# Tokenizer of a vision tower: the first two linear layers as one product of 512 columns over raw pixels and their std, with the weights loaded and combined ahead of the images

## The chip, the cores and the metric

The kernel runs on one core of one Trainium2 chip. A core has five engines that run side by side: TensorE (PE; its weight loads are shown as PEld), VectorE (DVE), ScalarE (ACT), GpSimd (POOL) and SyncE (SP), and 16 DMA engines that work off the transfers which SP, ACT and POOL issue. The metric is device time in microseconds; the time of a kernel is the median of its runs. All data is float32, and each matrix product of the program is two instructions on TensorE.

## The reference

Four images of 3 x 224 x 224 are cut into 8 x 8 patches: 784 tokens per image, 3136 in all, of 192 values each. What matters here is the tokenizer:

```python
def layernorm(x, g, b):
    mu = jnp.mean(x, axis=-1, keepdims=True)
    var = jnp.mean(jnp.square(x - mu), axis=-1, keepdims=True)
    return (x - mu) * jax.lax.rsqrt(var + EPS) * g + b
...
tokens = layernorm(patches, ln1_g, ln1_b)
tokens = tokens @ W1 + b1
tokens = layernorm(tokens, ln2_g, ln2_b)
q = tokens
k = tokens
tokens = jnp.concatenate([q, k, tokens], axis=1)
h1 = layernorm(tokens @ Wp1 + bp1, lnp_g, lnp_b)
h1 = jax.nn.silu(h1)
return h1 @ Wp2 + bp2
```

W1 is 192 x 256, Wp1 and Wp2 are 256 x 256, and EPS is 1e-5. The three copies of the tokens are equal, so the kernel computes one and writes it three times at the end. Behind the tokenizer come an attention over the images, a mixture of six experts with two chosen per token, a linear attention and a second mixture of four experts. The diff doesn't touch those.

## The kernel before

The 3136 tokens are 28 tiles of 112 rows (TT), taken in 7 groups of 4 tiles (GT). Inside a `manual_schedule` block the engines it names issue in the order in which the code is written; everywhere else, and for the engines not named, a planner chooses the order from modelled costs.

**Loading.** Lines 208 to 219 allot `img` (112 partitions, which are image and patch row; 32 rows of 224 pixels, of which 24 are pixels and 8 are zeros) and issue the four images by turns on SP and ACT, then the gain and shift of the first normalisation (ACT) and W1 (SP). Line 228 and the next load b1, spread over the partitions (POOL), Wp1 (SP) and bp1 (POOL). The small vectors of all layers are gathered as rows of `stage` by POOL (line 170) and turned into columns `cols` by one transpose (line 446). SP then loads the other weights and, once POOL has cleared `nothing` (line 249), writes zeros over `xrows` and `yrows` in device memory (line 253): 38 transfers of 1024 KB and two of 768.

**Turning the patches.** `turn_patches(k)` (line 342) turns 4 of the 28 patch columns: 32 small products against the identity per half, two halves, and a ScalarE copy into `pT` for each. After it VectorE takes the statistics of the same 4 columns (line 443). Ahead of k = 5 `first_layer` (line 357) multiplies the gain into W1, takes the mean over its rows off, adds the shift's part to b1 and permutes the rows of W1 to the order of `pT`. After k = 6 `patch_scales` (line 397) makes 1/std of every patch and brings it, by one product (`pr`, line 415), to the layout of the tokens. All of it is written in order for VectorE and TensorE (line 425).

**The tokenizer.** `tokenize(g)` (line 499) is a pipeline of three steps over groups. Step 1 for group g: the product with W1 (`pw`), times 1/std plus b1, statistics, rescaled rows `xn`. Step 2 for group g - 1: `turned_rows` transposes `xn` and applies ln2's gain and shift on ScalarE (`xTln_g`), the product with Wp1 (`pwp`), plus bp1, statistics, rescaled rows. Step 3 for group g - 2: transpose, lnp's gain and shift and Silu on ScalarE (`xTlnp_g`), the product with Wp2 (`pwp`), plus bp2 into `h`. Every product goes through `mm_rows` (line 312; its matmuls are at line 317), every transpose through `transposed` (line 292; line 297). Products use seven PSUM buffers of 512 columns in turn. Groups 0 to 6 are called at line 528, in the planner's order; `tokenize(7)` and `tokenize(8)`, which finish the last groups, stand in the hand-written block of line 1040, on either side of `keys_values(0)`. That function (line 1016) makes the attention's keys and values of a group (`pkv`), and `second_norm` the statistics it needs.

## Time and profile before

| | |
|---|---|
| median of 3 runs | 815.91 us (812.31 to 816.7) |
| profiled execution | 849.85 us |
| its span | 848.1 us |
| mean granted TensorE clock in it | 0.954 |
| busy in the span: PE, DVE, ACT, POOL | 88%, 61%, 38%, 15% |
| images landed, TensorE starts on them | 17.2 us |
| first product of the tokenizer | 39.3 us |
| first transposes for the keys | 136.4 us |

The profile is of one execution, and that one took longer than the runs. A row of the timeline gives start, length, engine, source line, operation, output and inputs, the number of instructions merged, and in brackets how long the engine sat idle before it and what ended that. "Line 317" is a helper's line, so products are told apart by their tiles. The page's table of 40 slices shows in its DMA row that the DMA engines are nearly saturated from the start until about 125 us: at first by the images and weights, then by the zeros.

### The profile page before, as it was taken

How to read it: one execution, taken by the hardware profiler on the slowest of the kernel's cores; microseconds unless marked ns; L12 is line 12 of the kernel's file. 1: busy time of each engine (PE TensorE's matmuls, PEld its weight loads, DVE VectorE, ACT ScalarE, POOL GpSimd, SP SyncE). 2: the span in 40 equal slices, each digit the busy share in tenths (PEclk: the TensorE clock that was granted, in tenths of full speed). 3: DMA queues.
4: the chain of work that ended last, by engine and by line, in shares of the span. 5: the costliest groups of instructions: out<-in, count | busy, mean ns of one | idle time of the engine just before them, and what ended most of it. 6: DMA issues, size and time to landing. Idle time of an engine off the chain costs nothing. (4 is left out here: it accounts for less than half of the span.)

```text
span 848.1 us, 11129 instructions
## 1 busy us (share of the span) xinstructions
PE 746.0 (88%) x3669; PEld 525.4 (62%) x3669; DVE 515.1 (61%) x1619; ACT 318.2 (38%) x758; POOL 129.3 (15%) x151
## 2 busy tenths in 40 slices
PE   2879988999788788799999999348999999999996
PEld 2758765555465466678878885335767675555553
DVE  4369886585787874346445655358995745544441
ACT  1333535455547573242222323323564612222221
POOL 5100000000024605430030022744000000000000
PEclk9999999999999988799999999759999999999999
DMA  8999990000001293332342224311000001333333
GB/s 197 360 421 419 419 384 0 1 0 1 1 22 55 82 367 95 103 127 75 100 131 88 94 88 137 93 52 55 1 2 0 1 3 27 100 101 101 99 100 100
DMA packets 58286, 97.52 MB, mean 115 GB/s; under 512 B 14590, under 2 KB 48564, under 8 KB 53364
## 3 DMA queue, kind: packets, MB, share of 16 engines
q1 hardware_dynamic: 51100, 80.78, 27.7%
q0 software_dynamic: 6224, 14.13, 5.8%
q10 hardware_dynamic: 904, 1.89, 0.9%
q8 instruction: 29, 0.48, 0.2%
q14 instruction: 29, 0.24, 0.1%
HBM read 31.04 MB, written 65.74 MB: 114 GB/s over the span
## 5 line engine op out<-in xcount | busy, mean ns | idle before, releaser
L901 POOL DMA_INDIRECT xrows<-xn,pos x56 | 59.9, 1070 | 282.4 <-ACT kq L665 233.2
L1369 POOL DMA_INDIRECT ys<-yrows,pos x56 | 54.3, 969 | 163.5 <-DMA yrows<-yb 134.0
L1173 PE MATMUL pb<-xTb,own 128*128 128x256 f32 x240 | 60.3, 396 | 7.0 <-DVE hb L1181 2.1
L1190 PE MATMUL pyb<-own,hb 128*128 128x256 f32 x240 | 59.4, 392 | 4.4 <-ACT hb L1179 4.4
L1173 PE MATMUL pb<-hb,own 128*128 128x256 f32 x240 | 58.8, 388 | 0.3 <-DVE hb L1181 0.3
L1179 ACT ACTIVATE hb<-pb,own 128x256 f32<-128x256 f32 x74 | 34.7, 473 | 61.7 <-PE pb L1173 42.1
L1173 PEld LDWEIGHTS pb<-xTb,own 128*128 128x128 f32 x240 | 45.5, 198 | 16.7 <-ACT xTb L1163 3.8
L1190 PEld LDWEIGHTS pyb<-own,hb 128*128 128x128 f32 x240 | 46.9, 197 | 12.0 <-ACT hb L1179 5.2
L297 PE MATMUL pt<-ident,xn 112*128 112x112 f32 x280 | 42.2, 281 | 12.4 <-DVE xn L482 6.9
L1574 PE MATMUL pqk<-Wqkv,lxT 128*112 128x512 f32 x112 | 50.0, 595 | 0.5 <-ACT lxT L81 0.5
L297 PEld LDWEIGHTS pt<-ident,xn 112*128 112x128 f32 x280 | 32.4, 148 | 26.4 <-issue 9.1
L1173 PEld LDWEIGHTS pb<-hb,own 128*128 128x128 f32 x240 | 44.5, 195 | 6.2 <-DVE hb L1181 0.7
L1196 DVE TENSOR_TENSOR yb<-pyb,eb 128x512 f32<-128x512 f32 x30 | 20.7, 691 | 45.5 <-PE pyb L1190 35.3
L306 PE MATMUL pe<-xT,eW 128*128 128x448 f32 x112 | 45.2, 546 | 0.0
L1648 PE MATMUL pukx<-xa,uk 112*128 112x258 f32 x112 | 29.0, 415 | 18.5 <-ACT uk L1606 18.5
L1163 ACT COPY xTb<-ptb 128x512 f32<-128x512 f32 x30 | 17.5, 583 | 73.8 <-PE ptb L1159 65.2
L1181 DVE TENSOR_SCALAR hb<-pb,own 128x256 f32<-128x256 f32 x46 | 22.2, 482 | 30.9 <-PE pb L1173 29.6
L1648 PEld LDWEIGHTS pukx<-xa,uk 112*128 112x128 f32 x112 | 22.7, 208 | 22.3 <-issue 18.8
L317 PE MATMUL pwo<-Wo,oT 128*112 128x256 f32 x112 | 29.0, 413 | 7.6 <-DVE oT L730 6.7
L1574 PEld LDWEIGHTS pqk<-Wqkv,lxT 128*112 128x112 f32 x112 | 19.2, 177 | 25.2 <-issue 22.7
L690 DVE SCALAR_TENSOR_TENSOR prod<-kq 128x784 f32<-128x784 f32 x32 | 30.4, 971 | 7.2 <-ACT kq L665 5.0
L1582 ACT ACTIVATE qk<-qk 112x256 f32<-112x256 f32 x56 | 22.8, 407 | 28.1 <-DVE qk L1578 23.8
(339 smaller groups left out, 1525.4 us busy)
## 6 DMA issues: line engine op xcount, KB each, us to landing
xrows<-nothing SPq DMA_DIRECT2D x19, 1024.0 KB
yrows<-nothing SPq DMA_DIRECT2D x19, 1024.0 KB
out_dram<-h SPq DMA_DIRECT2D x26, 336.0 KB
xb<-xrows SPq DMA_DIRECT2D x30, 256.0 KB
yrows<-yb SPq DMA_DIRECT2D x30, 256.0 KB
ew<-in_L_ffn_expert_w_dram SPq DMA_DIRECT2D x6, 768.0 KB
wb<-wd SPq DMA_DIRECT2D x28, 112.0 KB
img<-in_x_dram ACTq DMA_DIRECT2D x2, 588.0 KB
```

Source lines behind the costliest of these rows:

```text
L297: nc.tensor.transpose(pt[:, j * TT : (j + 1) * TT], xn[:, j, c * P : (c + 1) * P], ident[:TT, :TT])
L306: nc.tensor.matmul(pm[: wcols.stop - wcols.start, :n], w[:, c, wcols], xT(c), start=(c == 0), stop=(c == chunks - 1),)
L317: nc.tensor.matmul(pm[:, i, :], xT(c, t), w[:, c, :], start=(c == 0), stop=(c == chunks - 1))
L690: nc.vector.scalar_tensor_tensor(prod, qTs[s][:, o, :], 1.0, kT[:, o, t * SEQ : (t + 1) * SEQ], ALU.mult, ALU.mult, accum_out=atts[s][:, o ...
L901: put = nc.gpsimd.indirect_dma_start(out=xrows[:, :], out_offset=bass.IndirectOffsetOnAxis(ap=pos[:, k, t0 + j : t0 + j + 1], axis=0), in_ ...
L1173: nc.tensor.matmul(pm, wm[:, c, o * P : (o + 1) * P], src[:, c, :], start=(c == 0), stop=(c == 1),)
L1179: nc.scalar.activation(dst[:, o, :], pm, AF.Relu, bias=b)
L1190: nc.tensor.matmul(pm[:, t, :], src[:, c, t * P : (t + 1) * P], wm[:, c, :], start=(c == 0), stop=(c == 1),)
L1369: got = nc.gpsimd.indirect_dma_start(out=y[:, j, k, :], out_offset=None, in_=yrows[:, :], in_offset=bass.IndirectOffsetOnAxis(ap=pos[:, k, ...
L1574: nc.tensor.matmul(pqk, xT[:, c, cut(j, 1)], Wqkv[:, c, : 2 * D], start=(c == 0), stop=(c == 1),)
L1582: nc.scalar.activation(half, half, AF.Square, accum_out=ss[:, j, i : i + 1])
L1648: nc.tensor.matmul(pg, uks[u][:, k, c * P : (c + 1) * P], xas[u % 4][:, k, : D + 2], start=(j == 0), stop=(j == TPI - 1),)
```

## The change

The normalisation of a patch is (x - mean) / s with s = sqrt(var + 1e-5). The mean is already taken off through the weights. Now s is left in, too: the product of raw pixels with the first weights is s times what it was, b1 has to be multiplied by s, and the next normalisation takes s out again, if its epsilon is scaled by s squared. So each patch's s is written as one more row of `img` (row 24, pixel 7 of the patch), where `turn_patches` turns it along with the pixels, and b1 becomes the matching row of the weights. Then ln2's gain and mean are multiplied into Wp1 as well and both layers are combined: `Wall` holds W1's 256 columns, which serve only to take ln2's variance, and the 256 columns of W1 times Wp1.

- Loads: ln1, ln2, W1, b1 and Wp1 are issued on SP and ACT ahead of the images; bp1 on POOL ahead of the small vectors. ln2 leaves `stage`.
- `first_layers` replaces `first_layer`; it stands ahead of the first `turn_patches`, and also combines the two weights.
- `patch_stds(k)` stands ahead of `turn_patches(k)`, which now needs the std of its columns; `scaled_variances` takes the place of `patch_scales`.
- `first_rows` replaces steps 1 and 2: one product of 512 columns per tile, of which ScalarE copies the right half into `y` and VectorE takes statistics of the left; then scale and bp1 on `y`, statistics, rescaled rows. `y` has two buffers instead of one.
- The transposes and the evacuation of step 2 go. Silu's transposes of group g - 1 stand in iteration g, its third product in iteration g + 1, so `tokenize(8)` holds only a product.

The parts of the diff that carry it (removed functions are in the listing above):

```diff
+    tok = ctx.enter_context(ExitStack())
+    tokp = tok.enter_context(tc.tile_pool(name="tok", bufs=1))
+    bp1 = tokp.tile([TT, D], F32, tag="bp1", name="bp1")
+    nc.gpsimd.dma_start(out=bp1, in_=a["L0_tok_bp1"].partition_broadcast(TT))
...
+    ln1 = tokp.tile([2, PD], F32, tag="ln1", name="ln1")
+    ln2 = tokp.tile([4, P], F32, tag="ln2", name="ln2")
+    b1 = tokp.tile([1, D], F32, tag="b1", name="b1")
+    W1 = tokp.tile([KP, 2, D], F32, tag="W1", name="W1")
+    Wp1 = tokp.tile([P, 2, D], F32, tag="Wp1", name="Wp1")
+    nc.sync.dma_start(out=ln1[:1], in_=a["L0_tok_ln1_g"].unsqueeze(0))
+    nc.scalar.dma_start(out=ln2[:2], in_=a["L0_tok_ln2_g"].rearrange("(r p) -> r p", p=P))
+    nc.sync.dma_start(out=ln1[1:], in_=a["L0_tok_ln1_b"].unsqueeze(0))
+    nc.scalar.dma_start(out=ln2[2:], in_=a["L0_tok_ln2_b"].rearrange("(r p) -> r p", p=P))
+    nc.sync.dma_start(out=W1, in_=a["L0_tok_W1"].rearrange("(s p) n -> p s n", p=KP))
+    nc.scalar.dma_start(out=b1, in_=a["L0_tok_b1"].unsqueeze(0))
+    nc.scalar.dma_start(out=Wp1, in_=a["L0_tok_Wp1"].rearrange("(c p) n -> p c n", p=P))
     for b in range(NI):
         eng = nc.scalar if b % 2 else nc.sync
...
+    SROW = 3 * 32 + CY
...
+    def without_mean(w, n, dim):
+        pm = ps_tile("pmean")[:n, :D]
+        for i in range(2):
+            nc.tensor.matmul(pm, allones[:n, :n], w[:, i, :], start=(i == 0), stop=(i == 1))
+        for i in range(2):
+            nc.vector.scalar_tensor_tensor(
+                w[:, i, :], pm, -1.0 / dim, w[:, i, :], ALU.mult, ALU.add
+            )
+    def first_layers():
+        gb = tokp.tile([P, 8], F32, tag="gbT", name="gbT")
         pt = ps_tile("pgb")
+        nc.vector.memset(gb, 0.0)
         for i in range(2):
             nc.tensor.transpose(
                 pt[:KP, 2 * i : 2 * i + 2], ln1[:, i * KP : (i + 1) * KP], ident[:2, :2]
             )
+        nc.tensor.transpose(pt[:, 4:8], ln2, ident[:4, :4])
+        nc.vector.tensor_copy(gb[:KP, :4], pt[:KP, :4])
+        nc.vector.tensor_copy(gb[:, 4:], pt[:, 4:8])
+        g1, g2 = (lambda i: gb[:KP, 2 * i : 2 * i + 1]), (lambda c: gb[:, 4 + c : 5 + c])
+        bb = tokp.tile([P, 2, TT], F32, tag="bb", name="bb")
         W1g = tokp.tile([KP, 2, D], F32, tag="W1g", name="W1g")
+        W2 = tokp.tile([P, 2, D], F32, tag="W2", name="W2")
         for i in range(2):
+            nc.vector.tensor_scalar(W1g[:, i, :], W1[:, i, :], g1(i), None, ALU.mult)
+        without_mean(W1g, KP, PD)
+        pw = ps_tile("pbw")[:1, :D]
         for i in range(2):
             nc.tensor.matmul(
+                pw, gb[:KP, 2 * i + 1 : 2 * i + 2], W1[:, i, :], start=(i == 0), stop=(i == 1)
             )
         nc.vector.tensor_tensor(b1, pw, b1, ALU.add)
         pp = ps_tile("pwc").rearrange("p (i d) -> p i d", i=2)
         for i in range(2):
             for half in range(2):
                 nc.tensor.matmul(
                     pp[:, i, :], perm[:, half, i].rearrange("p g k -> p (g k)"),
+                    W1g[:, half, :], start=(half == 0), stop=(half == 1 and i == 0),
+                )
+        nc.tensor.matmul(pp[:, 1, :], srow, b1, start=False, stop=True)
+        Wall = tokp.tile([P, 2, 2 * D], F32, tag="Wall", name="Wall")
+        nc.vector.tensor_copy(Wall[:, :, :D], pp)
+        for c in range(2):
+            nc.vector.tensor_scalar(W2[:, c, :], Wp1[:, c, :], g2(c), None, ALU.mult)
+        for c in range(2):
+            nc.vector.tensor_copy(
+                bb[:, c, :], gb[:, 6 + c : 7 + c].to_broadcast([P, TT])
+            )
+        without_mean(W2, P, D)
+        WcT = tokp.tile([P, 2, 2 * P], F32, tag="WcT", name="WcT")
+        pt = ps_tile("pwct").rearrange("p (f k) -> p f k", f=2)
+        for f in range(2):
+            for i in range(2):
+                nc.tensor.transpose(
+                    pt[:, f, i * P : (i + 1) * P], Wall[:, i, f * P : (f + 1) * P], ident
+                )
+        nc.scalar.copy(WcT, pt)
+        pw = ps_tile("pbw2")[:TT, :D]
+        for c in range(2):
+            nc.tensor.matmul(pw, bb[:, c, :], Wp1[:, c, :], start=(c == 0), stop=(c == 1))
+        nc.vector.tensor_tensor(bp1, pw, bp1, ALU.add)
+        pp = ps_tile("pw2").rearrange("p (i d) -> p i d", i=2)
+        for i in range(2):
+            for f in range(2):
+                nc.tensor.matmul(
+                    pp[:, i, :], WcT[:, f, i * P : (i + 1) * P], W2[:, f, :],
+                    start=(f == 0), stop=(f == 1),
+                )
+        nc.vector.tensor_copy(Wall[:, :, D:], pp)
+        return Wall
+    def patch_stds(k):
+        w0 = k * GT
+        for w in range(w0, w0 + GT):
+            nc.vector.bn_stats(pst[:, w, :], img[:, :CY, w * PATCH : (w + 1) * PATCH])
+        st, v = pst[:, w0 : w0 + GT], pv[:, w0 : w0 + GT]
+        d = tokp.tile([TT, GT], F32, tag="pd", name="pd")
         nc.vector.tensor_tensor(d, st[:, :, 1], st[:, :, 4], ALU.subtract)
         nc.vector.tensor_tensor(v, st[:, :, 2], st[:, :, 5], ALU.add)
         nc.vector.scalar_tensor_tensor(d, d, PD / 4.0, d, ALU.mult, ALU.mult)
         nc.vector.tensor_tensor(v, v, d, ALU.add)
+        nc.scalar.activation(
+            img[:, CY, w0 * PATCH : (w0 + GT) * PATCH].rearrange("q (w x) -> q w x", x=PATCH)[
+                :, :, PATCH - 1
+            ],
+            v, AF.Sqrt, bias=eps[:TT], scale=1.0 / PD,
+        )
+    def scaled_variances():
+        nc.vector.tensor_scalar(pv, pv, 1e-5 / PD, 1e-10, ALU.mult, ALU.add)
...
+        Wall = first_layers()
         for k in range(HP // GT):
-            if k == 5:
-                W1g = first_layer()
+            patch_stds(k)
             turn_patches(k)
-            for w in range(k * GT, (k + 1) * GT):
-                nc.vector.bn_stats(pst[:, w, :], img[:, :CY, w * PATCH : (w + 1) * PATCH])
-        rtok = patch_scales(pst)
+        ev = scaled_variances()
...
+    def first_rows(g):
+        t0 = groups[g][0]
+        y = tokp.tile([TT, GT, D], F32, tag="y", name="y", bufs=2)
+        st = small.tile([TT, GT, 6], F32, tag="st", name="st")
+        mv = small.tile([TT, GT, 2], F32, tag="mv", name="mv")
+        for j in range(GT):
+            pm = ps_tile("pw1")[:TT]
+            for c in range(2):
+                nc.tensor.matmul(
+                    pm, pTf[:, c, cut(t0 + j, 1)], Wall[:, c, :], start=(c == 0), stop=(c == 1)
+                )
+            nc.scalar.copy(y[:, j, :], pm[:, D:])
+            nc.vector.bn_stats(st[:, j, :], pm[:, :D])
+            nc.vector.bn_aggr(mv[:, j, :], st[:, j, :])
+        r = small.tile([TT, GT], F32, tag="rstd", name="rstd")
+        nc.vector.tensor_tensor(r, mv[:, :, 1], ev[:, t0 : t0 + GT], ALU.add)
+        nc.scalar.activation(r, r, AF.Sqrt, bias=zero[:TT])
+        nc.vector.reciprocal(r, r)
+        st = small.tile([TT, GT, 6], F32, tag="st", name="st")
+        mv = small.tile([TT, GT, 2], F32, tag="mv", name="mv")
+        for j in range(GT):
+            nc.vector.scalar_tensor_tensor(
+                y[:, j, :], y[:, j, :], r[:, j : j + 1], bp1, ALU.mult, ALU.add
+            )
+            nc.vector.bn_stats(st[:, j, :], y[:, j, :])
+            nc.vector.bn_aggr(mv[:, j, :], st[:, j, :])
+        r = small.tile([TT, GT], F32, tag="rstd", name="rstd")
+        nc.scalar.activation(r, mv[:, :, 1], AF.Sqrt, bias=eps[:TT])
         nc.vector.reciprocal(r, r)
         xn = tokw.tile([TT, GT, D], F32, tag="xn", name="xn")
         for j in range(GT):
...
             )
         return xn
+    def turned_rows(xn):
+        xT = tokw.tile([P, 2, GN], F32, tag="xTt", name="xTt")
         def put(c, pt):
+            nc.scalar.activation(
+                xT[:, c, :], pt, AF.Silu, scale=col("lnp_g", c), bias=col("lnp_b", c)
+            )
         transposed(xn, GT, put)
         return xT
+    normed, third = {}, {}
     def tokenize(g):
+        if g < len(groups):
+            normed[g] = first_rows(g)
         if 1 <= g <= len(groups):
+            third[g - 1] = turned_rows(normed.pop(g - 1))
         if g >= 2:
+            sT = third.pop(g - 2)
             t2 = groups[g - 2][0]
+            for two in halves(range(GT)):
+                nc.vector.tensor_tensor(
+                    h[:, t2 + two[0] : t2 + two[0] + 2, :],
+                    mm_rows(two, lambda c, j: sT[:, c, cut(j, 1)], Wp2, "pwp2"),
+                    over(bp2, 2), ALU.add,
+                )
```

## The prediction

> **What bounds the kernel now.** I read the page's busy table first (TensorE busy 88% of 848.1 us), then the windows by stage, then the timeline inside the stages that the diff touches. Columns of the windows: length, busy time (instructions) of PE, PEld, DVE, ACT and POOL, granted TensorE clock, DMA share, GB/s.

> ```profile
> 17.20:39.30 22.10, 18.58 (x469) 16.74 (x469) 11.62 (x44) 9.06 (x16) 7.11 (x11) 1.00 1.01 339
> 39.30:64.90 25.60, 20.87 (x90) 15.77 (x90) 16.37 (x58) 7.47 (x11) 0.00 (x0) 0.87 1.01 422
> 64.90:114.90 50.00, 48.65 (x257) 39.89 (x256) 42.23 (x137) 22.37 (x32) 0.00 (x0) 1.00 1.01 420
> 114.90:136.30 21.40, 18.27 (x81) 13.98 (x80) 16.98 (x59) 7.60 (x12) 0.00 (x0) 0.92 0.50 205
> 136.30:150.40 14.10, 11.73 (x49) 7.34 (x48) 8.20 (x25) 6.38 (x11) 0.00 (x0) 1.00 0.00 0
> ```

> Between 64.9 and 114.9 the tokenizer keeps TensorE busy 97% of the time: TensorE sets its pace. Before and after that stretch it has gaps, and the clock sinks to 0.87 and 0.92. So two kinds of time can go: TensorE work in the middle, gaps at both ends. One period of the middle, on PE:

> ```profile
> 93.35 3.62 PE L317 MATMUL pwp<-Wp,xTlnp_g 128*112 128x256 f32 x16
> ...
> 96.81 0.93 PE L297 MATMUL pt<-ident,xn 112*128 112x112 f32 x8
> ...
> 98.08 0.41 PE L297 MATMUL pt<-ident,xn 112*128 112x112 f32 x2 [0.34 <-DVE xn L482]
> ...
> 99.39 3.19 PE L317 MATMUL pw<-Wc,pT 128*112 128x256 f32 x14
> ...
> 102.41 3.62 PE L317 MATMUL pwp<-Wp,xTln_g 128*112 128x256 f32 x16
> ...
> 105.86 3.62 PE L317 MATMUL pwp<-Wp,xTlnp_g 128*112 128x256 f32 x16
> ```

> From start to start the period is 105.86 - 93.35 = 12.51 us: three products of 16 instructions at 3.46 (102.41 to 105.86; 0.216 each) are 10.4, and 16 transposes with one short wait are 2.1. The ends:

> ```profile
> 17.23 10.80 PE L347 MATMUL ptp<-ident,img 112*32 112x112 f32 x320 [14.26 <-DMA img<-in_x_dram]
> ...
> 38.75 0.38 PE L415 MATMUL pr<-div,rr 112*112 112x28 f32 x2 [2.21 <-DVE rr L410]
> ...
> 39.34 5.38 PE L317 MATMUL pw<-Wc,pT 128*112 128x256 f32 x16
> ...
> 127.53 5.53 PE L317 MATMUL pwp<-Wp,xTln_g 128*112 128x256 f32 x16 [2.33 <-ACT xTln_g L492]
> ...
> 146.71 3.89 PE L317 MATMUL pwp<-Wp,xTlnp_g 128*112 128x256 f32 x16 [1.89 <-ACT xTlnp_g L492]
> ```

> Sixteen instructions that take 3.46 in the middle take 5.38 and 5.53 after a gap; windows of 2 us show a granted clock of 0.50 at 40 to 42, 60 to 62 and about 128 to 131, each spell costing some 1.7 us. From the first product (39.34) to the transposes of the first keys (136.35) are 97.0 us. Warm work in them is 20 products x 3.46 + 14 sets of transposes x 0.8 = 80.4; the other 16.6 are gaps and cold spells.

> **Part 1: from start to first product (now 39.34).** W1 (192 KB), Wp1 (256 KB) and bp1 (112 KB) go ahead of the images, 560 KB. At the 173 GB/s of the windows up to 17.2 that is 3.3 us, at the 339 of the weights' stretch 1.7; the image DMAs also stand behind three issues on SP and four on ACT of some 0.42 each. So the images land 1.6 to 5 us after today's 17.2; I take 2.7, thus 19.9: the rows near it are weight loads.

> first_layers has no row. Its first half, with the weights' old form, ran from 27.96 to 34.0 on a warm TensorE (6.05 us with 16 instructions). The new one has 34 instructions of 256 columns (0.22 warm, 0.43 at half clock), some 6.2 us of VectorE edits (0.34 to 0.75 each by the rows of 28 to 34 us) and a ScalarE copy, mostly one after another. Twice 6.05 is 12.1; with a cold first half 15.6. Step by step I get 13.9. It starts when VectorE is through its constants (now 7.1, then 7.4), so it ends at 21.3, 1.4 after the images. So it is hidden but for 1.4, and its old place (5.3 us of TensorE between chunks) is freed.

> bp1 is queued on POOL. A small load of that queue, issued at 4.23, let its waiter go only at 14.55:

> ```profile
> 14.55 0.53 POOL L170 DMA_DIRECT2D stage<-in_L_ffn_sb_dram  x1 [5.76 <-DMA stage<-in_L_tok_ln_g_dram]
> ```

> So bp1 lands about 13 to 15, before VectorE adds to it at about 19; were it over 6 us later, the images' std would wait behind that add. The stage loads move one POOL issue back (0.5) and are needed only after the last chunk.

> Each patch_stds then adds a wait: turn_patches(k) needs row 24 of the image, so 4 bn_stats (0.27 each), four tiny VectorE operations (36.12 to 36.79: 0.67), a root (0.32) and hops. The first chunk starts 2.2 after 21.3, at 23.5. Then VectorE (1.73 per k) is just slower than TensorE (1.54): six more k are 10.4, the last chunk and its copy 2.3, a cold start 0.8. First product at **37.0**. patch_scales' 2.2 us wait is gone: scaled_variances is ready while TensorE still turns the last chunk. **Gain 2.3** (between -3 and 5).

> **Part 2: the tokenizer (now 97.0).** One product of 512 columns replaces two of 256. Its row is layer 1's:

> ```profile
> 664.73 5.15 PE pqk L1574 x12
> ```

> 0.43 each, so 6.87 for 16: as long as the two it replaces (6.92). What goes is 8 of 16 transposes per group (0.8), the wait between first and second product, and ln2's evacuation. Work: 7 x 6.87 + 6 x 3.46 + 7 x 0.8 = 74.5.

> Off TensorE, VectorE now spends 42.23 / 50 x 12.51 = 10.6 us per group; it loses the sum with bp1 (2 x 0.66) and four rescalings (4 x 0.345) and gains one tiny addition: 8.1 of an 11.1 us period. ScalarE gains four copies of 256 columns (0.37 to 0.40, by L1582's 402 ns and L665's 486 for 392), loses two evacuations (1.34): two roots, two Silu and two table loads stay, 6.0 in all. Neither sets the pace. [...]

> [...] first_rows reads each product with ScalarE and with VectorE. No row of before has such a pair. [...]

> [...] This trace has:

> ```profile
> 73.79 1.28 ACT L492 ACT_TABLE_LOAD   x1
> ...
> 75.08 1.34 ACT L492 ACTIVATE xTlnp_g<-pt,cols 128x448 f32<-128x448 f32 x2
> ```

> The next operation starts 1.29 after the load: the row decides. [...]

> The chain behind a group's last product: bn_stats 0.6 (+0.5), root and reciprocal 0.9, four scalings and statistics 3.9, second root 0.8 (perhaps a load 1.28), rescaling 1.4: 8.1 us, with a load 9.4. In the middle it lies beside the next product (6.87), one set of transposes and the third layer (3.46), 11.1 in all. It sticks out at the start, where only product 1 covers group 0 (8.1 - 6.9 = 1.2), and at the end, where group 6 has only one set of transposes and one third layer beside it (8.1 to 9.4 less 4.3; I take 4.1). With one cold spell of 1.7 the losses are 7.0, against 16.6 now. Together 81.5: **gain 15.5** (5.9 if the losses stay, 22.5 if none remain).

> **Part 3: tokenize(8).** Its transposes, table load and Silu are now one step earlier, so after the first keys (143.88) the third layer starts at once: 150.43 - 143.88 - 3.46 = **3.1 gained**. The wait before it goes; late next is the product of the second keys, on TensorE itself.

> **Sum.** 2.3 + 15.5 + 3.1 = 20.9, span 827.2. Nothing later absorbs it: the stages up to 260 us are TensorE's (98.57 of 109.6), and the zero fill of xrows (to about 125 us) is waited for only by much later scatters. The profiled execution took 849.85 around its span, with a clock of 0.954, while the median of the runs is 815.91, 0.96 of it. (827.2 + 1.75) x 0.96 = **796**.

> **The rivals.**
> - *Root behind copies* (15%): only VectorE and TensorE are in written order. If ScalarE puts root k+1 behind the copies of chunk k, a step is 1.54 + 0.2 + 0.54 + 0.4 = 2.7, the first product at 42: 801. For: nothing written holds the root ahead. Against: in this trace a root (37.71) stands ahead of the last copy (37.94).
> - *Gaps stay* (12%): cold spells and waits as large as today's; only transposes go: 20.9 - 9.6 = 11.3, 805. For: the new chain has two roots and more steps than either old one. Against: it is one chain per group, where there were two.
> - *Slower* (6%): the copies sit on ScalarE behind a Silu that waits for the group before, so product and chain no longer overlap: 6.9 + 8.1 + 0.8 = 15.8 per group, 6 x 4.7 = 28 more, 823. It decides from 11.1 + 20.9 / 6 = 14.6 per group. Against: today's order overlaps chains of the same kind with a 0.34 wait.
> - *Nothing measurable* (4%): the same mechanism near its deciding point, about 816.

> **Numbers.** Forecast 63%, alone 787 (losses 0 to 2, product at 35) to 803. The range 787 to 809 takes in the first two rivals and leaves out the last two. Faster 0.90, within 0.5% 0.04, slower 0.06; half a per cent is about what these runs can tell from no change.

> **What would show it.** Right: first product at 36 to 38; PE period near 11.1; no xTln_g rows; third layer directly after pkv. Wrong: images after 22; gaps between chunks over 1 us; a period above 12.5; bn_stats waiting on ACT y.

## The result, and the profile after

| kernel | median of runs | the kernel before beside it | ratio, 95% interval |
|---|---|---|---|
| changed | 808.78 us (806.16 to 810.82) | 812.39 us | 0.9952 (0.9933 to 0.9971) |

The change is worth 3.6 us, where 20 were forecast. The sign is right and the time lies just inside the range, but most of the gain is missing. The profiled execution took 810.54 us, its span is 808.8. Here and below a median is over all runs, while a ratio leaves out runs more than 1.5% above the fastest of their kernel.

The windows of the changed kernel by stage (columns as before: length, busy time and instructions of PE, PEld, DVE, ACT and POOL, granted clock, DMA share, GB/s):

```profile
7.30:25.00 17.70, 15.78 (x41) 9.80 (x41) 4.70 (x17) 0.59 (x1) 6.97 (x11) 1.00 1.00 228
25.00:51.10 26.10, 15.48 (x452) 14.34 (x451) 12.24 (x60) 10.35 (x22) 0.00 (x0) 0.87 1.01 421
51.10:66.80 15.70, 15.70 (x34) 6.17 (x33) 8.29 (x34) 3.29 (x10) 0.00 (x0) 0.89 1.01 420
66.80:123.00 56.20, 56.20 (x208) 32.38 (x208) 41.93 (x150) 42.63 (x62) 0.00 (x0) 1.00 1.01 420
123.00:137.80 14.80, 7.98 (x27) 5.85 (x26) 10.25 (x37) 7.58 (x11) 0.00 (x0) 0.65 0.04 17
```

The middle of the tokenizer is what was forecast: TensorE is busy for all of 66.8 to 123. The second row is the surprise. Turning the patches takes 26.1 us, in which TensorE is busy for 15.5, VectorE for 12.2 and ScalarE for 10.4: no engine is full, and only the DMA engines are. The timeline of TensorE shows how it spends them:

```profile
24.98 1.22 PE L356 MATMUL ptp<-ident,img 112*32 112x112 f32 x38
28.28 3.77 PE L356 MATMUL ptp<-ident,img 112*32 112x112 f32 x136 [2.08 <-ACT img L452]
35.36 6.05 PE L356 MATMUL ptp<-ident,img 112*32 112x112 f32 x128 [3.31 <-issue]
42.93 3.33 PE L356 MATMUL ptp<-ident,img 112*32 112x112 f32 x128 [1.51 <-issue]
49.95 0.74 PE L356 MATMUL ptp<-ident,img 112*32 112x112 f32 x18 [3.69 <-issue]
...
51.11 15.68 PE L517 MATMUL pw<-Wall,pT 128*112 128x512 f32 x32
...
112.03 7.03 PE L517 MATMUL pw<-Wall,pT 128*112 128x512 f32 x16
...
130.11 2.07 PE L300 MATMUL pt<-ident,xn 112*128 112x112 f32 x8 [6.82 <-DVE xn L540]
131.97 5.95 PE L320 MATMUL pwp<-Wp,xTt 128*112 128x256 f32 x16
137.76 0.93 PE L300 MATMUL pt<-ident,xn 112*128 112x112 f32 x8
...
145.29 3.62 PE L320 MATMUL pwp<-Wp,xTt 128*112 128x256 f32 x16
148.74 0.93 PE L300 MATMUL pt<-ident,xn 112*128 112x112 f32 x8
```

The turning has 448 matmul instructions, two for each of 224 small products (16 products per half, hence 32 instructions; the description of `turn_patches` calls the instructions products), and each has a weight load. Once the stds are there (28.28), TensorE still stands three times, 8.5 us in all, each time released by "issue", which means by nothing that the profile shows. The stands fall behind matmul 174, 302 and 430, in the middle of a half of 32, where the program waits for nothing. Between two stands lie exactly 128 matmuls, which are 256 instructions with their weight loads, and the starts are 7.6 and 7.0 us apart. After the first stand the 128 matmuls take 6.05 us instead of 3.33, at a granted clock of 0.52 (35.3 to 41.4 us). So the first product of the tokenizer starts at 51.11. The two groups at the end of the list are the transposes of the first keys (137.76; 136.35 before) and of the second ones (148.74; 150.43 before).

What comes in at the pace of the stands is seen in the DMA view. In three stretches of one microsecond, from 33, 40 and 47 us, it lists one packet of an instruction queue, and no other of that queue between 25 and 50 us (the share of the third is 5.8%):

```profile
q8 instruction: 1, 0.02, 5.5%
```

Columns: packets, MB, share of the 16 engines. On the profile's page the queue's 28 packets are 0.46 MB, so one is 16 KB. If it holds the 256 instructions between two stands, that is 64 bytes each by this estimate; 28 times 256 are 7168, and TensorE has 7048 recorded instructions (3524 matmuls and as many weight loads), so the queue is very probably its own. TensorE went on 2.2 to 2.5 us after the start of each packet. Around these packets the zero fill, which SP began to issue at 23.4 us, takes the DMA engines whole (share 1.01, 421 GB/s).

### The profile page after: what moved, and what is told of

Its sections match the earlier page's. It is cut to its first block, busy times and chain, and to the rows that moved or that the text cites. A ratio compares the mean times of both kernels' runs of the same rounds, so it can differ in the third digit from the quotient of the medians.

```text
span 808.8 us, 10871 instructions
## 1 busy us (share of the span) xinstructions
PE 739.7 (91%) x3524; PEld 501.2 (62%) x3524; DVE 504.0 (62%) x1618; ACT 334.1 (41%) x789; POOL 131.0 (16%) x148
## 5 line engine op out<-in xcount | busy, mean ns | idle before, releaser
L1415 POOL DMA_INDIRECT ys<-yrows,pos x56 | 57.2, 1021 | 141.9 <-DMA yrows<-yb 125.8
L1219 PE MATMUL pb<-hb,own 128*128 128x256 f32 x240 | 57.1, 380 | 0.3 <-DVE hb L1227 0.3
L1236 PE MATMUL pyb<-own,hb 128*128 128x256 f32 x240 | 57.0, 380 | 0.2 <-ACT hb L1225 0.2
L1219 PEld LDWEIGHTS pb<-xTb,own 128*128 128x128 f32 x240 | 44.6, 194 | 12.5 <-ACT hb L1225 1.9
L517 PE MATMUL pw<-Wall,pT 128*112 128x512 f32 x112 | 51.0, 610 | 0.0
L300 PE MATMUL pt<-ident,xn 112*128 112x112 f32 x224 | 34.6, 286 | 12.5 <-DVE xn L540 6.8
L300 PEld LDWEIGHTS pt<-ident,xn 112*128 112x128 f32 x224 | 27.0, 151 | 26.9 <-ACT xn L824 9.5
L517 PEld LDWEIGHTS pw<-Wall,pT 128*112 128x112 f32 x112 | 20.1, 182 | 26.2 <-issue 22.9
L1628 ACT ACTIVATE qk<-qk 112x256 f32<-112x256 f32 x56 | 22.8, 407 | 27.7 <-DVE qk L1624 25.2
## 6 DMA issues: line engine op xcount, KB each, us to landing
ew<-in_L_ffn_expert_w_dram SPq DMA_DIRECT2D x6, 768.0 KB, 11.4
```

The costliest lines, as they stand in the source:

```text
L300: nc.tensor.transpose(pt[:, j * TT : (j + 1) * TT], xn[:, j, c * P : (c + 1) * P], ident[:TT, :TT])
L517: nc.tensor.matmul(pm, pTf[:, c, cut(t0 + j, 1)], Wall[:, c, :], start=(c == 0), stop=(c == 1))
L1219: nc.tensor.matmul(pm, wm[:, c, o * P : (o + 1) * P], src[:, c, :], start=(c == 0), stop=(c == 1),)
L1236: nc.tensor.matmul(pm[:, t, :], src[:, c, t * P : (t + 1) * P], wm[:, c, :], start=(c == 0), stop=(c == 1),)
L1415: got = nc.gpsimd.indirect_dma_start(out=y[:, j, k, :], out_offset=None, in_=yrows[:, :], in_offset=bass.IndirectOffsetOnAxis(ap=pos[:, k, ...
```

## Experiments

The experiments ran on three chips, whose times differ: before took 812.2 us beside the first four, 851.7 beside the next four and 850.4 beside the last four. Ratios compare between them, run times in microseconds only within one. The first product and the marker come from one trace per kernel and are set side by side across chips too: after_late has 39.69 and 141.82 on the first chip, 39.22 and 140.98 on the third, so differences below a microsecond are not read. As a marker in the traces I use the start of the first query products (`pq`): 157.91 in the trace of before that the prediction used, 156.04 in another execution of the same part (before_late below), 156.22 after the change. Against that other trace of before the change gains nothing at the marker (0.2 later), while the runs show 3.6 us: a trace is one execution.

| kernel | median | ratio to before, 95% | first product | marker |
|---|---|---|---|---|
| after_late | 796.55 | 0.9805 (0.9769 to 0.9840) | 39.69 | 141.82 |
| before_late | 812.35 | 1.0001 (0.9980 to 1.0022) | 39.66 | 156.04 |
| after_small | 822.26 | 1.0116 (1.0082 to 1.0151) | 50.06 | 167.52 |
| before_early | 811.72 | 0.9993 (0.9974 to 1.0011) | 38.24 | 159.56 |
| late_k5 | 853.32 | 0.9973 (0.9937 to 1.0009) | 53.65 | 157.01 |
| late_tail | 835.66 | 0.9797 (0.9754 to 0.9841) | 39.40 | 138.75 |
| late_stds | 837.51 | 0.9831 (0.9790 to 0.9872) | 36.49 | 139.88 |
| late_both | 833.01 | 0.9777 (0.9738 to 0.9816) | 37.50 | 133.80 |
| before_fill17 | 853.31 | 1.0040 (1.0013 to 1.0067) | 48.69 | 165.03 |
| late_warm | 825.35 | 0.9701 (0.9664 to 0.9738) | 34.00 | 131.99 |
| late_both2 | 827.60 | 0.9736 (0.9696 to 0.9776) | 36.36 | 132.66 |
| after_late2 | 834.49 | 0.9806 (0.9769 to 0.9844) | 39.22 | 140.98 |

### Take the fill away from the turning: after_late

```diff
-    nothing = tokp.tile([P, 8 * D], F32, tag="nothing", name="nothing")
-    nc.gpsimd.memset(nothing, 0.0)
...
+    nothing = tokw.tile([P, 8 * D], F32, tag="nothing", name="nothing", bufs=1)
+    cleared = nc.gpsimd.memset(nothing, 0.0)
+    tc.add_manual_dep(
+        cleared.ins, turned_last[0].ins.name,
...
+    )
     for r in range(0, XROWS, 8 * P):
```

The new lines stand behind the block that turns the patches, and `turned_last[0]` is the copy of the last of them.

> The changed kernel, but the zero fill of xrows and yrows is issued only once the last turned patches are copied (cleared memset on POOL waits for that copy). Theory fill (TensorE waits for its own instructions, which come by DMA behind the fill's packets): the three stands released by 'issue' (3.3, 1.5 and 3.7 us) and the clock spell behind them go, the first product starts at 36 to 39 instead of 51.1, the kernel takes 795 to 800 us, 0.983 to 0.989 of the changed one. Rival roots (VectorE's statistics and ScalarE's roots set the turning, as each chunk needs its stds): the first product stays at 48 to 51, time within 2 us of the changed kernel's.

TensorE's timeline of after_late:

```profile
24.03 1.23 PE L349 MATMUL ptp<-ident,img 112*32 112x112 f32 x38
27.33 7.05 PE L349 MATMUL ptp<-ident,img 112*32 112x112 f32 x264 [2.08 <-ACT img L445]
34.79 3.32 PE L349 MATMUL ptp<-ident,img 112*32 112x112 f32 x128 [0.41 <-issue]
38.52 0.74 PE L349 MATMUL ptp<-ident,img 112*32 112x112 f32 x18 [0.41 <-issue]
...
39.69 13.99 PE L524 MATMUL pw<-Wall,pT 128*112 128x512 f32 x32
...
116.99 2.07 PE L291 MATMUL pt<-ident,xn 112*128 112x112 f32 x8 [6.82 <-DVE xn L547]
118.85 4.72 PE L311 MATMUL pwp<-Wp,xTt 128*112 128x256 f32 x16
123.41 0.93 PE L291 MATMUL pt<-ident,xn 112*128 112x112 f32 x8
```

The stands shrink from 8.5 to 0.8 us, with the same wait for the stds before them (2.08) and the same VectorE work (12.29 us busy, 12.24 after the change): theory fill holds, and rival roots falls as the cause of the stands. The instruction packets now come in the stretches 28 to 30, 32 to 34 and 34 to 36 us, near 28.3, 32.1 and 35.9: 3.8 us apart, which is TensorE's own pace (3.32 for 128 matmuls and a stand of 0.41). The kernel takes 796.55 us, 12.2 less than the changed one; beside them the kernel before took 812.2 and 812.4. The marker comes 14.4 earlier. 13.1 of that are the fill's: 11.4 at the first product (51.11 to 39.69) and 1.7 in its slow start (15.68 to 13.99; the granted clock is 0.50 from 52 to 54 us in the changed kernel, 1.00 here). The other 1.2 lie in the last third layer (5.95 to 4.72), behind a wait of 6.82 in both traces. They are not the fill's: late_k5 and late_stds below, whose fill is late too, have 5.95 and 5.97 there.

### The same for the kernel before: before_late

The same edit on the kernel before.

> The kernel before with the zero fill put off in the same way. Theory fill: there only the last 128 of the 448 turning matmuls stood beside the fill, so little is to be had: within 3 us of the kernel before, first product at 38 to 39.5. Rival (putting the fill off is worth much by itself, whatever the change): 10 us or more faster than before.

No difference. TensorE's timeline of before_late:

```profile
17.26 7.55 PE L340 MATMUL ptp<-ident,img 112*32 112x112 f32 x218 [14.30 <-DMA img<-in_x_dram]
25.61 2.73 PE L340 MATMUL ptp<-ident,img 112*32 112x112 f32 x102 [0.80 <-issue]
```

444 recorded instructions of TensorE go ahead of this stop (222 matmuls with their weight loads), and 438 ahead of the first stand after the change. That is nearer to two blocks of 256 than to any other number of them, so two blocks, it seems, lay at hand when the images landed. In the trace of before the queue's first packet comes between 22 and 24 us, ahead of the fill (from 25.2), and the second between 28 and 30, while TensorE is at first_layer's few long instructions. By the count these two serve the rest of the turning (940 recorded instructions to its end, 444 and 512 are 956), although 230 of its 448 matmuls start behind the fill. So the fill in its place was harmless until the change: it spends 76 instructions on first_layers before the patches are turned, and moves the turning, with the fetching of its blocks, to where the fill runs.

### Packets of 1 KB: after_small

```diff
-                out=rows_[r : r + n * P, :].rearrange("(p k) d -> p (k d)", k=n),
-                in_=nothing[:, : n * D],
+                out=rows_[r : r + n * P, :].rearrange("(k p) d -> p k d", k=n),
+                in_=nothing[:, : n * D].rearrange("p (k d) -> p k d", k=n),
```

> The changed kernel with the fill in its place, but written in runs of 1 KB instead of up to 8 KB. Theory fill, by packet size (an instruction packet waits behind long packets): stands by 'issue' shrink to under 1 us each, first product at 38 to 43. By share (any saturated DMA does it): stands stay, first product 48 to 52. Rival roots: no difference from the changed kernel.

The stands stay (3.10, 3.97 and 1.39, again 8.5), so the size of the fill's packets isn't what holds a block up. The fill, now at 338 to 348 GB/s, lasts until 147 us, and that brought something not expected. ScalarE's timeline of after_small, and its row for the same operation in the changed kernel:

```profile
132.01 1.34 ACT L550 ACTIVATE xTt<-pt,cols 128x448 f32<-128x448 f32 x2
147.65 1.34 ACT L1067 ACTIVATE mT<-pt,cols 128x448 f32<-128x448 f32 x2 [14.30 <-issue]
```

```profile
138.39 1.34 ACT L1067 ACTIVATE mT<-pt,cols 128x448 f32<-128x448 f32 x2 [4.00 <-issue]
```

ScalarE stood 14.3 us, to the end of the fill within a microsecond. Some 4 of them stand in the changed kernel as well, where it waits for the transposes; the other 10 are new, and TensorE waited 10.8 us for `mT` (0.5 after the change). It looks like the same thing on another engine, but no instruction packet of this moment is in the trace, so that stays an inference.

### The fill beside the turning in the kernel before: before_early and before_fill17

before_early queues the fill ahead of the attention weights. before_fill17 also clears its source earlier, between the small loads on POOL:

```diff
+        if i == 9:
+            nc.gpsimd.memset(nothing, 0.0)
         nc.gpsimd.dma_start(out=stage[r0 : r0 + n, :width], in_=src)
```

> The kernel before, with the fill ahead of the attention weights in SP's queue, so that it starts some 4 to 6 us earlier, beside most of the turning. Theory fill: stands by 'issue' of 1.5 to 4 us appear in the turning of the kernel before, first product at 43 to 50 instead of 39.3, 3 to 9 us slower than before. Rival roots: no stands, first product at 38 to 40, within 2 us of before.

> The kernel before, with the fill's source cleared and its DMAs queued early enough that the fill runs from about 17 us, beside the whole turning (before_early moved its start by only 1.4 us). Theory fill (TensorE's instructions come in blocks of 256 by DMA, and under the fill one takes about 7 us): the first some 220 turning matmuls run from what was fetched while TensorE waited for the images, then stands by 'issue' of 2 to 4 us appear in the kernel before too; first product at 43 to 50 instead of 39.5, 3 to 9 us slower than before. Rival (the stands need the changed kernel, whose first_layers uses up fetched instructions): no stand over 1 us, first product at 38 to 41, within 1.5 us of before.

before_early told nothing: SP still waited for POOL to clear `nothing`, so the fill began at 23.8 us instead of 25.2, and no stand appeared. In before_fill17 it runs from 16.7. TensorE's timeline:

```profile
16.85 7.13 PE L348 MATMUL ptp<-ident,img 112*32 112x112 f32 x218 [13.88 <-DMA img<-in_x_dram]
27.39 5.09 PE L348 MATMUL ptp<-ident,img 112*32 112x112 f32 x102 [3.41 <-issue]
...
35.09 1.91 PE L379 MATMUL pw1m<-W1g,allones 96*96 96x256 f32 x4
...
48.69 3.71 PE L318 MATMUL pw<-Wc,pT 128*112 128x256 f32 x16
```

The stand appears in the kernel before, after 218 matmuls as forecast, and the half clock behind it (0.50 from 27 to 43 us) stretches everything up to 41 us (`pw1m` 1.91; 1.03 before). So the stand needs no first_layers ahead of it. The first product comes at 48.69 and the marker 9 us later than in before_late, which ran on another chip. The runs show only 0.4%, some 3 us, at the lower end of the 3 to 9 forecast. On the first chip the part behind the marker, with the changed kernel's trace, is the same to within 1.9 us (652.1 to 654.0); on this one it is 687.5 here and 694.5 in after_late2. What returned the difference was not pursued.

### Put the weights back behind the images: late_k5

after_late with the images first in the queues, and `first_layers` at its old place, ahead of k = 5.

```diff
         for k in range(HP // GT):
+            if k == 5:
+                Wall = first_layers()
             patch_stds(k)
```

> After_late with the change's 'weights ahead' undone: the images first in the queues again, and first_layers again ahead of the sixth chunk. Theory (weights ahead is worth its 2 to 3 us: its time on TensorE is hidden under the images' transfer): images land at about 17 instead of 19.4, but first_layers stands in the turning with 8 to 11 us, first product at 41 to 44 instead of 39.7, 2 to 4 us slower than after_late. Rival (weights ahead gives back what it takes: the images' delay and the cold TensorE cost as much): first product at 38 to 40, within 1.5 us of after_late.

Both sides were far off: the first product comes 14 us later in the trace, and by the runs the new product without the earlier weights isn't told apart from the kernel before (0.9973). TensorE's timeline of late_k5:

```profile
26.98 3.95 PE L349 MATMUL ptp<-ident,img 112*32 112x112 f32 x102 [2.01 <-issue]
...
32.02 1.99 PE L363 MATMUL pmean<-W1g,allones 96*96 96x256 f32 x4 [0.73 <-DVE W1g L386]
...
35.73 3.78 PE L397 MATMUL pwc<-W1g,perm 96*128 96x256 f32 x8
...
53.65 13.99 PE L525 MATMUL pw<-Wall,pT 128*112 128x512 f32 x32
```

From 31 to 47.6 us TensorE does first_layers, at half clock (granted clock 0.50 from 30 to 44), behind a stand of 2 us. That is 16.5 us in the open, where the change hides nearly all of it under the images' transfer. The stand comes without a fill: other loads take the DMA engines whole from 22 to 24 us (336 GB/s, share 1.06), and TensorE stands from 24.97 to 26.98, behind 218 matmuls as in before_fill17. So a stand of this kind needs no fill; that a block came late beside those loads is my inference. The traced execution took 857.48 us, and the 14 runs reach from 844.10 to 857.96, so the 14 us, the stand and its half clock are those of a long one. That there is a loss, the runs say (0.9973 against 0.9805).

### The end of the tokenizer: late_tail

ScalarE's timeline of the changed kernel at its end:

```profile
120.16 1.28 ACT L550 ACT_TABLE_LOAD   x1 [0.69 <-PE pt L300]
121.45 0.73 ACT L550 ACTIVATE xTt<-pt,cols 128x448 f32<-128x448 f32 x1
122.20 1.28 ACT L525 ACT_TABLE_LOAD   x1
123.49 0.30 ACT L525 ACTIVATE rstd<-rstd,zero 112x4 f32<-112x4 f32 x1
123.81 1.28 ACT L550 ACT_TABLE_LOAD   x1
125.10 0.72 ACT L550 ACTIVATE xTt<-pt,cols 128x448 f32<-128x448 f32 x1
125.84 1.28 ACT L536 ACT_TABLE_LOAD   x1
127.77 0.30 ACT L536 ACTIVATE rstd<-mv,eps 112x4 f32<-112x4 f32 x1 [0.64 <-DVE mv L534]
```

VectorE's rows for the input of the first root and for the reciprocal behind the second:

```profile
120.20 0.16 DVE L524 TENSOR_TENSOR rstd<-mv,ev 112x4 f32<-112x4 f32 x1
129.37 0.14 DVE L537 RECIPROCAL rstd<-rstd 112x4 f32<-112x4 f32 x1
```

The two halves of group 5's Silu and the two roots of group 6 alternate, with a table load between each. The first root's input is there at 120.36, but it runs at 123.49, behind the first Silu half: 3.1 us in the chain that the end hangs on. Behind the second root (to 128.07) VectorE does statistics of the first keys before the reciprocal: 1.3 more. late_tail writes the last iteration by hand, for ScalarE too: first root, Silu, second root; third layer of group 5 ahead of the transposes of group 6; the first keys' statistics ahead of all.

```diff
+    with tc.manual_schedule(engines={ENG.DVE, ENG.PE, ENG.Activation}):
+        stats0 = ln_stats(lambda j: h[:, groups[0][0] + j, :], GT, twice=True, own="0")
+        normed[last] = first_rows(last, turned, lambda: third_sums(last - 2, pms[0]))
+        pms[1] = third_products(last - 1)
...
-        second_rows(0, second_norm(0))
-        tokenize(len(groups))
+        second_rows(0, stats0)
+        third[last] = turned_rows(normed.pop(last))
+        third_sums(last - 1, pms[1])
```

> After_late with the last group's order on VectorE, TensorE and ScalarE written by hand: its first root ahead of the Silu of group 5, the third layer of group 5 ahead of the transposes of group 6, the statistics of the first keys before all of it. Theory tail (the 2 to 3 us that the end of the tokenizer took over the prediction are ScalarE's switching of tables between roots and Silu, and VectorE's second_norm ahead of the last reciprocal): TensorE's stand of 6.8 us before group 6's transposes goes to 0 to 2 us, transposes of the first keys at 115 to 118 instead of 123.4, 5 to 8 us faster than after_late. Rival (the chain behind the last product is long in itself): transposes of group 6 no earlier than 116, under 2 us gained.

Rows of TensorE, of late_tail and then of late_both:

```profile
114.08 2.87 PE L292 MATMUL pt<-ident,xn 112*128 112x112 f32 x16 [0.36 <-DVE xn L552]
118.66 6.31 PE L301 MATMUL pkv<-mT,Wk 128*128 128x448 f32 x8 [1.71 <-ACT mT L1103]
```

```profile
116.75 3.27 PE L301 MATMUL pkv<-mT,Wk 128*128 128x448 f32 x8 [1.70 <-ACT mT L1105]
```

The transposes of group 6 and of the first keys now run together from 114.08, behind a stand of 0.36 instead of 6.8. But the marker gains only 3.1: after a wait of 1.7 the first keys' product took 6.31 us instead of 3.27. In late_both, with the same wait, it took 3.27, and the marker stands 6.1 ahead of late_stds. So the new order takes the wait away, and a spell at half pace (the 6.31 for 3.27) can take half of the gain back: by its runs late_tail (0.9797) isn't told apart from after_late (0.9805). It changes three things together, so what each is worth alone isn't shown.

### The stds ahead, all together, and a warm TensorE: late_stds, late_both, late_warm

late_stds puts `patch_stds(0)` behind the mean of W2 in first_layers. late_both has both edits. late_warm adds, ahead of first_layers:

```diff
+        warm = ps_tile("warm")
+        for i in range(20):
+            nc.tensor.matmul(warm[:, (i % 4) * P : (i % 4 + 1) * P], allones, ident, start=True, stop=True)
         Wall = first_layers()
```

> After_late with patch_stds(0) ahead of the last part of first_layers on VectorE. Theory: the 2.1 us that TensorE waits for the first stds (2.08 <-ACT img) go, and the turning keeps its pace of VectorE: first product at 37.5 to 38.5 instead of 39.7, 1 to 2 us faster. Rival (VectorE sets the pace of the turning anyway): within 0.5 us.

> Late fill, hand-written end and patch_stds(0) ahead, together. If their gains add: 787 to 790 us, about 0.969 of the kernel before; if they lie on the same wait: no faster than the better of late_tail and late_stds.

> Late_both with 20 products of 128 columns (allones by ident, into a PSUM tile that nothing reads) on TensorE while it waits for W1, ahead of first_layers. Theory cold (first_layers took 17.7 us instead of my 13.9 because TensorE came from idle and ran at half speed): its products of 256 columns take 0.25 instead of 0.47 to 0.5 us each, first_layers ends 3 to 5 us earlier, the images' transfer then bounds it, first product at 34 to 35.5 instead of 37, 2 to 3 us faster than late_both. Rival (the short stops of first_layers keep TensorE at half speed, whatever ran before): no change beyond 0.5 us, or slower by the instructions that it uses up.

> Late_both once more, beside the other kernels of this call on one chip. Theory: 6 to 8 us faster than after_late, as the marker in the traces (the first query products, 133.8 against 141.8 us) says.

> After_late once more, on the same chip as late_both2 and late_warm: 0.978 to 0.983 of the kernel before.

late_stds did all 448 matmuls of the turning in 12.19 us without a stop, and its first product came 3.2 us earlier; by its runs alone (0.9831) it isn't told apart from after_late either. Together the gains add in the traces: the marker of late_both is 8.0 ahead of after_late's. Its runs on the second chip (0.9777) missed the forecast (0.969) and don't tell it apart from after_late (0.9805); with both on the third chip the medians differ by 6.9 us (834.49 to 827.60), and no run of one lies in the range of the other. TensorE's timeline of late_warm:

```profile
2.89 7.27 PE L493 MATMUL warm<-ident,allones 128*128 128x128 f32 x40
...
11.04 1.10 PE L364 MATMUL pmean<-W1g,allones 96*96 96x256 f32 x4 [0.64 <-DVE W1g L387]
...
13.03 1.99 PE L398 MATMUL pwc<-W1g,perm 96*128 96x256 f32 x8
...
34.00 13.99 PE L532 MATMUL pw<-Wall,pT 128*112 128x512 f32 x32 [0.23 <-ACT pT L355]
```

first_layers starts almost 3 us later and ends over 3 us earlier than in after_late, with each of its products at half the time (`pwc` 1.99 for 8; 3.78 after the change). So the length of first_layers was that of a TensorE at half pace. At 0.9701 of before it is by its median the fastest kernel of this study, 2.3 us ahead of late_both2 beside it, though the runs of the two overlap; the changed one is at 0.9952.

## Why the prediction was wrong

Up to the transposes of the second keys I had summed a gain of 20.9 us; the profile shows 1.7 (150.43 to 148.74). The missing 19.2, by the steps of the prediction:

- **"Nothing later absorbs it", with the zero fill counted by who waits for its end.** This is the step that failed: 13.1 of the 19.2. No instruction waits for the fill, but the fill holds up TensorE's instructions: three stands of 8.5 us in the turning, which go when the fill is put off (0.8 in after_late). The views of before had half of it: the DMA row was full from the start, and matmuls of some 26 ns (3.33 us for 128) use up 256 instructions in 3.3 us. The stands themselves didn't show there, since, by the counts under before_late, two blocks lay at hand and the next two came in time.
- **first_layers at 13.9 us.** Measured 17.7, and 16.7 without the fill; the first chunk came at 24.0 instead of 21.3 in after_late: 2.7. I had 15.6 for a cold first half and went by 13.9, step by step; it ran at half pace for nearly all of its length (late_warm shows what full would be: 9.8 us from the product for its first mean to the turning, 16.8 in the changed kernel). That it hides under the images was right, and the images landed at 19.4 (19.9 forecast), bp1 at 12.96 (13 to 15).
- **The turning behind the stds.** The wait is 2.08 (2.2 forecast), and from there the turning without the fill kept the forecast pace. VectorE, forecast just the slower one, is level with TensorE: in the changed kernel its statistics of the chunks start 1.64 us apart (25.70, 27.34 and so on to 35.56; 1.73 forecast), with VectorE busy for 1.9 of every 2 us, and TensorE takes 3.33 for the 128 matmuls of two chunks (1.54 forecast for one). In late_stds TensorE does all seven without a stop in 12.19, 1.74 each.
- **The middle.** Period 11.09 to 11.10, as worked out; TensorE has no gap there. Of the losses of 7.0, after_late shows 9.2: 0.3 at the start instead of 1.2, a wait of 6.8 at the end instead of 4.1, and 2.1 at a sunken clock behind it (0.68 from 116 to 124 us) instead of 1.7. The end is ScalarE's order, which I had given one table load, and VectorE's statistics ahead of the last reciprocal: the root rival's mechanism, behind Silu instead of copies and at the other end. That is 2.2 in after_late, and 3.4 in the changed kernel, whose last third layer took 1.2 longer (5.95; granted clock 0.61 from 132 to 138 us); why the clock comes back sooner or later is open.
- **tokenize(8).** 3.1 forecast, 3.1 measured (14.08 to 10.98 between the first and second keys' transposes).

13.1 + 2.7 + 3.4 = 19.2. That after_late takes 796.55 us, as forecast, is partly chance: its runs gain 15.6 and not 20, but on a before of 812.2 instead of 815.9. The trace of before that the sum started from was itself 1.9 late at the marker, by a slow first product (5.38, with the clock at 0.50 from 40 to 42 us; 3.71 in before_late).

What the sum assumed: the 0.5 beside bn_stats, on each of the two exposed chains, was an estimate for a bn_stats that starts only behind ScalarE's copy of the same buffer. After the change bn_stats of a first product started at 55.12 (the idle time before it ended by `<-ACT y`), when ScalarE's copy of the same buffer (54.72, 0.37 long) had ended. A semaphore orders that, so it doesn't show what would happen without. On table loads the row of before held: the first root follows 1.29 us after the start of its load (122.20 to 123.49).

## What to carry to other kernels

A transfer that nobody waits for isn't free while an engine works through many short instructions (here 8.5 us of stands): count instructions per microsecond against the pace at which they come in (here 256 in 7.0 to 7.6 us under a fill of 421 GB/s, used up in 3.3), and start the fill when TensorE has long ones, as after_late does: its products of 512 columns ran beside the fill without a gap (44.0 us busy of 44.0). Work put into an idle stretch of an engine also takes the start that the engine had there, here 76 of the instructions at hand, and it ran at half pace itself (`pwc` 3.78 us; 1.99 in late_warm); price what stood in the idle time's shadow. And where a chain is the last of its kind, with nothing behind it to hide its waits, look at the order on each engine that it crosses, because a planner's order that costs nothing in the middle costs its full length there.

## What the runs showed that I had not expected

- The granted clock on record and the pace differ: from 7.3 to 25 us the changed kernel's record says 1.00, while up to 22 us 256 columns took 0.47 to 0.5 us, as at 0.50 in late_k5 (`pwc` 3.78 for 8 in both). In 9 us with hardly a stop (8.18 to 16.83) it didn't recover; after 7.3 us of unbroken products it was at full pace (late_warm: `pmean` 1.10 for 4 instead of 1.99). What makes the difference no run here shows.
- Whether TensorE goes on at half pace after a stand isn't set by its length alone. After 3.31 us 128 matmuls took 6.05 instead of 3.33, and after 2.01 (late_k5) they were slow, too (3.95 for 102; granted clock 0.57 from 28 to 30 us); after 2.08 (3.77 for 136), and after 3.10 in after_small (3.32 for 128), they ran at full pace. Between the stands the slow pace cost nothing, since the next block sets the start; behind the last one it cost the first product 1.7 us (15.68; 13.99 in after_late).
- A prolonged fill stopped ScalarE for 14.3 us at one place, some 10 more than without, on a stretch with few instructions.
